# A two-layer graph transformer kernel: edge lags kept, one tile's output products moved, first loads re-ordered

## The chip, the core and the metric

The kernel runs on one core of a Trainium2 chip. The core has five engines that run side by side, each through its own list of instructions in order: TensorE (PE, matrix products into the accumulators in PSUM), VectorE (DVE), ScalarE (ACT), GpSimd (POOL) and SyncE (SP). SP, ACT and POOL also start DMA transfers between the chip's memory and the on-chip buffer SBUF. An engine waits for another through semaphores.

The metric is the device time of one execution in microseconds (us). Three executions of the kernel before took 2208.89, 2213.21 and 2214.76 us; the median is 2213.21.

## The reference, cut to what matters

There are 625 nodes of 1024 features and 10000 edges. Each of two layers normalises the nodes, adds a graph part and a linear attention to them, and then adds a feed-forward part. All that the change touches lies in layer 0:

```python
edge_index = jnp.stack([src, dst])
xn = _layernorm(x, axis=-1)
x = x + _L0_gnn_ref(xn, edge_index, L0_gnn_rms_w, ...) + _L0_mix_ref(xn[None], L0_mix_W_q, ...)[0]
x = x + _L0_ffn_ref(_layernorm(x, axis=-1)[None], L0_ffn_w_gate, ...)[0]
xn = _layernorm(x, axis=-1)
...
# _L0_gnn_ref: attention along the edges, 4 heads of 64
xl = (x @ Wl).reshape(n, H, D)
xr = (x @ Wr).reshape(n, H, D)
msg = xl[src] + xr[dst]
act = jnp.where(msg > 0, msg, NEG_SLOPE * msg)
e = jnp.einsum('ehd,hd->eh', act, att)
m = jax.ops.segment_max(e, dst, num_segments=n)
p = jnp.exp(e - m[dst])
denom = jax.ops.segment_sum(p, dst, num_segments=n)
alpha = p / (denom[dst] + 1e-16)
out = jax.ops.segment_sum(alpha[..., None] * xl[src], dst, num_segments=n)
return out.reshape(n, HID) @ W_up
# _L0_mix_ref: linear attention, 16 heads of 64
kv = jnp.einsum('bhnd,bhne->bhde', kf, v)
denom = jnp.einsum('bhnd,bhd->bhn', qf, ksum) + EPS
out = jnp.einsum('bhnd,bhde->bhne', qf, kv) / denom[..., None]
return out.transpose(0, 2, 1, 3).reshape(B, N, D_MODEL) @ W_o + b_o
```

## The kernel before

**Tiles.** The 625 nodes are five tiles of 125 rows. Nodes transposed (`xnT`, `oT`) have features on the partitions in eight chunks of 128. Weights of 1024 x 1024 come in halves of 512 columns, and a `Half` (L113) loads one half as two transfers of 1 MB on SP's queue. The pool `wpool` has six such 1 MB buffers. The engines' order is the order in which the program calls them: nothing is scheduled afterwards. `Stream` (`do`, L174) only delays: what follows a product on DVE or ACT (`after`) is recorded when the next product is asked for.

**Opening.** The rows of x are loaded by SP, and W_down, then the left and right weights of the edge attention. ACT starts the loads of src, dst, rms_w and att at once. For each tile DVE normalises (`norm`, L485), PE transposes and makes the down product, and ACT writes the left and right rows (`xlr`) to the memory buffers `xl_d` (started by ACT) and `xr_d` (started by POOL). `root` (L496) makes a scale with a square root on ACT between two small DVE steps. A buffer `table` in memory takes one value per head for every pair of nodes, and SP fills it with zeros from a constant (6160 KB). The key and value weights of layer 0 come after these zeros in SP's order. A transfer that SP or ACT starts takes one of eight completion counters, in turn, and before it starts waits until the last transfer on that counter has landed. So a transfer on one queue can wait for one on another.

**Edges.** The 10000 edges stand 128 at a time in 79 columns, in 40 groups of two columns (the last has one of 16). For a column, POOL gathers the left rows (`ga`, by src) and the right rows (`gb`, by dst), DVE adds and scores them (`score_group`, L596), ACT raises them to exponentials, and POOL scatters the column to `table` (`scatter`, L605). Every scatter waits for the one before it to land, as both write `table`. The rows wait in five buffers on each side.

**Beats.** These steps are laid among the attention's products by a clock of estimated PE time: every product calls `work(us)`, and once enough has passed a beat is recorded (`one_beat`, L663). In beat g POOL gathers group g, DVE scores group g − 4, ACT raises g − 5 and POOL scatters g − 6 and g − 7's rest; these are the `lags` 4, 5, 6 (L650). The first six beats are 5.2 us apart, the others 8.5. Beats 5 to 9 also make the self loops of a tile and store them in the table's diagonal. Between two scatters of a beat stand gathers.

**Attention, layer 0.** First keys and values (L0_Wk, L0_Wv), with a product that counts edges into a matrix `CT` between them; then per 128 columns m a query product and, one step later, `answer` (L327): two products `pd`, `po`, and on DVE a sum, a reciprocal and a multiplication into `oT`. In the last two steps of that loop all lags are lowered by one each time. `mixed(t)` (L718) makes tile t's products with W_o, two halves of eight chunks, into a two-bank accumulator `px1` of the tag `ps2`, which has three buffers. Tile 0's first six chunks are made before the last answer. Then tiles 3 and 4 are finished and kept in SBUF (`kept`, with the bias), and 0, 1 and 2 stay in their accumulators. On the way DVE sums and rounds the feed-forward weights to three values (`weight_sums`, `ternary`).

**Tile periods.** When all edges are scattered, `load_table` (L807) reads the table's columns of a tile back (started by POOL, 1.25 MB), `weigh` multiplies them with `CT` on DVE, `sums` makes the weighted sums on PE, `up_again` multiplies with W_up into the tile's accumulator (for tiles 3 and 4 into a fresh one) and DVE adds that to x. The loop over p (L1025) overlaps this for tile p with the feed-forward of tile p − 1 (`ffn`) and, from p = 2 on, with layer 1's key and value products as spacers. Before it POOL starts the load of table tile 0, of all five row tiles of x, and of table tile 1. SP's loads of layer 1's key and value weights stand at p = 1.

Of the kernel before, what the change touches and what calls it, by code (L numbers as in the profile page):

```python
# [21 lines left out]
P = 125  # L22
NP = 626
HN = 313
E = 10000
# [28 lines left out]
def attempt(ctx: ExitStack, tc: tile.TileContext, w: dict, out: bass.AP, shifted: bool):  # L54
# [161 lines left out]
    class LinearAttention:  # L216
# [17 lines left out]
        def half(self, c, loaded=False):  # L234
            Wk, bk, Wv, bv = (w[n] for n in self.names[1:])
            self.bk, self.bv = self.bias(bk, c, "bk_t"), self.bias(bv, c, "bv_t")
# [107 lines left out]
    with ExitStack() as st0:  # L344
# [8 lines left out]
        with ExitStack() as edges:  # L353
# [10 lines left out]
            for dst, name in ((si, "src"), (di, "dst")):  # L364
                flat = w[name].rearrange("a b -> (a b)")
                nc.scalar.dma_start(out=dst[:, 0:EF], in_=flat[0:128 * EF].rearrange("(p t) -> p t", t=EF))
                nc.scalar.dma_start(out=dst[0:ER, EF:EN], in_=flat[128 * EF:E].rearrange("(p t) -> p t", t=1))
# [5 lines left out]
            for t in range(2, NT):  # L373
# [5 lines left out]
            nc.scalar.dma_start(out=att, in_=w["att"].to_broadcast([128, 256]))  # L379
# [5 lines left out]
            nc.gpsimd.memset(none, FAR if shifted else 0.0)  # L385
            nc.sync.dma_start(out=table.rearrange("(p a b) h -> p a (b h)", p=128, a=28),
                              in_=none.unsqueeze(1).to_broadcast([128, 28, 440]))
            sf = pool.tile([128, EN], FP, name="sf")
# [5 lines left out]
            def edge_numbers():  # L394
                for dst, src in ((sf, si), (df, di)):
                    nc.vector.memset(dst[:, EF:EN], -1.0)
                    nc.vector.tensor_copy(dst[:, 0:EF], src[:, 0:EF])
                    nc.vector.tensor_copy(dst[0:ER, EF:EN], src[0:ER, EF:EN])
# [11 lines left out]
            if not shifted:  # L410
                nc.vector.tensor_scalar(att, att, 0.8, None, op0=ALU.mult)
# [128 lines left out]
            turn_x(1)  # L540
            root(0)
            for t in range(NT):
# [9 lines left out]
                if t == NT - 2:  # L552
# [4 lines left out]
            lin = LinearAttention(xnT, ("L0_Wq", "L0_Wk", "L0_bk", "L0_Wv", "L0_bv"), w["L0_bq"],  # L557
                                  lambda us: work(us), nc.sync)
            lin.half(0)
# [121 lines left out]
            def work(us):  # L681
                beat["us"] += us

                while beat["us"] >= 2.0 + 5.2 * min(beat["g"], 6) + 8.5 * max(beat["g"] - 6, 0) and chunks:
# [33 lines left out]
            def mixed(t, ks=range(KC), keep=None, then=None):  # L718
                for c in range(2):
# [15 lines left out]
                    work(0.87 * len(ks))  # L735
# [29 lines left out]
            for m in range(KC):  # L765
                if m >= KC - 2:
# [1168 lines left out]
```

## Time and profile before

| | |
|---|---|
| three executions, median | 2213.21 us (2208.89 to 2214.76) |
| the profiled execution, whole | 2212.67 us |
| its span, first to last instruction | 2210.6 us |
| PE busy | 2119.9 us (96%) |
| DVE, ACT, POOL busy | 714.3, 194.3, 342.3 us |
| mean granted clock of PE | 0.978 |
| first gather on POOL | 53.47 us |
| last scatter on POOL | 409.18 us |
| load of the first table tile issued | 414.73 us |
| first table product on DVE | 424.29 us |

Times in the views are us from the span's start. A row of the order of time gives start, duration, engine, line, operation, output and input with their shapes; in brackets stand the engine's idle time before it and what ended that. A row of the waits gives the engine and what it was about to do, then who released it, then total, number and longest. The granted clock is the share of full speed that PE was given. A busy PE is not a PE at its peak, since matrix products are pipelined. An f32 product of one chunk is two records.

### The profile page before, as it was taken

What the parts mean: (1) busy time and instruction counts of PE and PEld (TensorE: products, weight loads), DVE (VectorE), ACT (ScalarE), POOL (GpSimd) and SP (SyncE); (2) the same over time, 40 slices, a digit from 0 to 9 for tenths busy, and PEclk for the clock granted to TensorE, in tenths of its full rate; (3) what the DMA queues carried; (4) which work ended last, traced back from release to release, by engine and by line L of the source; (5) the groups of instructions that cost most, each with busy time, mean ns of one, the idle gap of its engine ahead of it and who ended that gap; (6) DMA issues with size and microseconds to landing.
All of it is one profiled execution on the core that took longest, in us unless ns stands there. A gap on an engine that the chain in (4) does not pass through costs nothing. (4 is left out here: it accounts for less than half of the span.)

```text
span 2210.6 us, 17366 instructions
## 1 busy us (share of the span) xinstructions
PE 2119.9 (96%) x6934; PEld 1215.4 (55%) x6934; DVE 714.3 (32%) x1216; ACT 194.3 (9%) x354; POOL 342.3 (15%) x351
## 2 busy tenths in 40 slices
PE   7999997869899989999999999999999999999998
PEld 5665573445455667754446767457744444444443
DVE  4786486467421760000122133322011111111012
ACT  2010110002211200000000111100000000000000
POOL 1666776400000120010000000110000000000011
PEclk9999999869999999999999999999999999999999
DMA  9335432620122110240213111122099988997742
GB/s 293 92 98 180 146 113 79 161 66 22 44 80 76 48 48 1 76 161 20 76 38 105 38 39 38 29 95 94 8 361 345 331 306 295 330 330 285 275 143 92
DMA packets 145849, 301.62 MB, mean 136 GB/s; under 512 B 12371, under 2 KB 22437, under 8 KB 145755
## 3 DMA queue, kind: packets, MB, share of 16 engines
q1 hardware_dynamic: 123412, 243.18, 31.0%
q0 software_dynamic: 17664, 47.47, 7.1%
q10 hardware_dynamic: 4678, 9.72, 1.4%
q8 instruction: 58, 0.95, 0.2%
q14 instruction: 37, 0.30, 0.0%
HBM read 277.49 MB, written 22.84 MB: 136 GB/s over the span
## 5 line engine op out<-in xcount | busy, mean ns | idle before, releaser
L130 PE MATMUL pu<-w,xgT 128*128 128x512 f32 x768 | 333.9, 593 | 1.9 <-DVE xgT L1229 1.9
L130 PEld LDWEIGHTS pu<-w,xgT 128*128 128x128 f32 x768 | 144.0, 190 | 174.8 <-issue 171.9
L130 PE MATMUL pyb<-w,hb 128*128 128x512 f32 x384 | 174.3, 598 | 2.5 <-ACT yb L105 2.1
L130 PE MATMUL pk<-w,xnT 128*125 128x512 f32 x320 | 143.9, 603 | 3.8 <-DMA w<-in_L_Wk_dram 3.2
L130 PE MATMUL pv<-w,xnT 128*125 128x512 f32 x320 | 141.2, 594 | 0.0
L130 PE MATMUL pq<-xnT,w 128*128 128x313 f32 x512 | 138.1, 428 | 2.0 <-ACT qf L320 1.2
L130 PE MATMUL p<-tT,w 128*128 128x313 f32 x512 | 136.3, 428 | 0.4 <-DVE tT L1229 0.4
L130 PEld LDWEIGHTS pyb<-w,hb 128*128 128x128 f32 x384 | 69.8, 189 | 90.9 <-issue 74.8
L130 PEld LDWEIGHTS pq<-xnT,w 128*128 128x128 f32 x512 | 96.5, 190 | 42.1 <-ACT qf L320 3.7
L1769 DVE TENSOR_TENSOR su<-pu,su 128x512 f32<-128x512 f32 x24 | 16.6, 692 | 314.6 <-ACT su L1768 314.6
L130 PEld LDWEIGHTS p<-tT,w 128*128 128x128 f32 x512 | 96.8, 190 | 37.9 <-issue 1.2
L130 PEld LDWEIGHTS pk<-w,xnT 128*125 128x125 f32 x320 | 60.3, 191 | 77.8 <-issue 76.0
L130 PEld LDWEIGHTS pv<-w,xnT 128*125 128x125 f32 x320 | 60.0, 189 | 72.4 <-issue 71.8
L610 POOL DMA_INDIRECT table<-es,at x79 | 83.9, 1062 | 63.2 <-issue 33.7
L1752 POOL DMA_INDIRECT xg<-rows_d,slots x12 | 11.4, 947 | 524.7 <-PE pxg L1759 449.0
L592 POOL DMA_INDIRECT ga<-xl_d,si x79 | 82.3, 1041 | 29.6 <-issue 19.8
L592 POOL DMA_INDIRECT gb<-xr_d,di x79 | 78.9, 998 | 24.1 <-issue 23.5
L724 PE MATMUL px<-w,oT 128*125 128x512 f32 x160 | 71.1, 605 | 11.3 <-DVE z L337 11.3
L1119 DVE TENSOR_TENSOR z<-pz,z 125x512 fp32r<-125x512 f32 x10 | 6.9, 692 | 196.8 <-ACT z L1117 196.8
L130 PE MATMUL px<-w,hT 128*125 128x512 f32 x160 | 70.3, 592 | 0.0
L130 PE MATMUL px<-w,oT 128*125 128x512 f32 x160 | 70.3, 592 | 0.0
L130 PE MATMUL ph<-meanT,w 128*128 128x313 f32 x256 | 70.0, 426 | 0.0
(368 smaller groups left out, 2538.9 us busy)
## 6 DMA issues: line engine op xcount, KB each, us to landing
w<-in_eW_dram SPq DMA_DIRECT2D x144, 1024.0 KB
w<-in_L_Wk_dram SPq DMA_DIRECT2D x8, 1024.0 KB
w<-in_L_Wv_dram SPq DMA_DIRECT2D x8, 1024.0 KB
w<-in_L_Wq_dram SPq DMA_DIRECT2D x8, 1024.0 KB
w<-in_L_Wo_dram SPq DMA_DIRECT2D x8, 1024.0 KB
w<-in_W_self_dram SPq DMA_DIRECT2D x8, 1024.0 KB
w<-in_W_neigh_dram SPq DMA_DIRECT2D x8, 1024.0 KB
w<-in_sW_dram SPq DMA_DIRECT2D x8, 1024.0 KB
```

The source lines that it names most:

```text
L130: nc.tensor.matmul(dst, lhsT=lhsT, rhs=rhs, start=(i == 0), stop=(i == len(pairs) - 1))
L592: nc.gpsimd.indirect_dma_start(out=ab[g][side][0:p, j, :], out_offset=None, in_=src[:, :], in_offset=bass.IndirectOffsetOnAxis(ap=ix[0:p, ...
L610: nc.gpsimd.indirect_dma_start(out=table[:, :], out_offset=bass.IndirectOffsetOnAxis(ap=at[0:p, lo + j:lo + j + 1], axis=0), in_=es[0:p, l ...
L724: nc.tensor.matmul(hold["px", t][:P, c, :], lhsT=oT[:, k, nodes(t)], rhs=wo[c](k), start=(k == 0), stop=(k == KC - 1 and keep is not None))
L1119: nc.vector.tensor_tensor(low, src, high.bitcast(FP), op=ALU.subtract)
L1752: nc.gpsimd.indirect_dma_start(out=xg, out_offset=None, in_=rows_d[:, :], in_offset=bass.IndirectOffsetOnAxis(ap=slots[:, b:b + 1], axis=0))
L1769: nc.vector.tensor_tensor(su, pu[:, 0, :], su, op=ALU.mult)
```

## The change

- `LinearAttention` for layer 0 is made earlier, and its biases and key weights are loaded ahead of the table's zeros, the value weights behind them (`biases`, and `half` with `biased`).
- The loads of src, dst and att (ACT's queue) move from the start behind the second tile's transpose (`load_edges`), and DVE's scaling of att into `edge_numbers`.
- A beat after the sixth is 8.1 us of estimated time instead of 8.5.
- The lags stay at 4, 5, 6 to the end of the loop over m, and are then set to 1, 1, 2 as before. Tile 0's six chunks before the last answer call no `work`.
- `kept` holds tile 3 only. Tile 0's last two chunks come right behind tile 3, and tile 4's products move to p = 1, one half before the sums of tile 1 and one after the table product of tile 2. They stay in an accumulator until p = 4, and tile 4's bias is added to x.
- Layer 1's first key and value weights are asked for behind the second half of these products.
- The second table tile is loaded behind the first row tile instead of the fifth.

```diff
+        def biases(self, c):
+            self.bk, self.bv = (self.bias(w[self.names[i]], c, tag) for i, tag in ((2, "bk_t"), (4, "bv_t")))
+
+        def half(self, c, loaded=False, biased=False):
+            if not biased:
+                self.biases(c)
...
-            for dst, name in ((si, "src"), (di, "dst")):
-                flat = w[name].rearrange("a b -> (a b)")
-                nc.scalar.dma_start(out=dst[:, 0:EF], in_=flat[0:128 * EF].rearrange("(p t) -> p t", t=EF))
-                nc.scalar.dma_start(out=dst[0:ER, EF:EN], in_=flat[128 * EF:E].rearrange("(p t) -> p t", t=1))
...
-            nc.scalar.dma_start(out=att, in_=w["att"].to_broadcast([128, 256]))
+
+            def load_edges():
+                for dst, name in ((si, "src"), (di, "dst")):
+                    flat = w[name].rearrange("a b -> (a b)")
+                    nc.scalar.dma_start(out=dst[:, 0:EF], in_=flat[0:128 * EF].rearrange("(p t) -> p t", t=EF))
+                    nc.scalar.dma_start(out=dst[0:ER, EF:EN], in_=flat[128 * EF:E].rearrange("(p t) -> p t", t=1))
+                nc.scalar.dma_start(out=att, in_=w["att"].to_broadcast([128, 256]))
...
+            lin = LinearAttention(xnT, ("L0_Wq", "L0_Wk", "L0_bk", "L0_Wv", "L0_bv"), w["L0_bq"],
+                                  lambda us: work(us), nc.sync)
+            lin.biases(0)
+            lin.wk = Half(wpool, w["L0_Wk"], 0)
             nc.sync.dma_start(out=table.rearrange("(p a b) h -> p a (b h)", p=128, a=28),
                               in_=none.unsqueeze(1).to_broadcast([128, 28, 440]))
+            lin.wv = Half(wpool, w["L0_Wv"], 0)
...
             turn_x(1)
+            load_edges()
             root(0)
...
-            lin = LinearAttention(xnT, ("L0_Wq", "L0_Wk", "L0_bk", "L0_Wv", "L0_bv"), w["L0_bq"],
-                                  lambda us: work(us), nc.sync)
-            lin.half(0)
+            lin.half(0, loaded=True, biased=True)
...
-                while beat["us"] >= 2.0 + 5.2 * min(beat["g"], 6) + 8.5 * max(beat["g"] - 6, 0) and chunks:
+                while beat["us"] >= 2.0 + 5.2 * min(beat["g"], 6) + 8.1 * max(beat["g"] - 6, 0) and chunks:
...
-            def mixed(t, ks=range(KC), keep=None, then=None):
-                for c in range(2):
+            def mixed(t, ks=range(KC), keep=None, then=None, paced=True, cs=(0, 1)):
+                for c in cs:
...
-                    work(0.87 * len(ks))
+                    if paced:
+                        work(0.87 * len(ks))
...
             for m in range(KC):
-                if m >= KC - 2:
-                    lags[:] = [n - 1 for n in lags]
                 if m + 1 < KC:
                     lin.query(m + 1)
                 else:
-                    mixed(0, range(6))
+                    mixed(0, range(6), paced=False)
...
-            kept = mid([P, 2, 2, 512], "kept")
-            mixed(3, keep=kept[:, 0], then=weight_sums)
-            mixed(4, keep=kept[:, 1])
+            kept = mid([P, 2, 512], "kept")
+            mixed(3, keep=kept, then=weight_sums)
+            mixed(0, range(6, KC))
             weight_means()
-            mixed(0, range(6, KC))
...
-            kept_apart = t >= 3
+            kept_apart = t == 3
...
             rows_dma(nc.gpsimd, x[:, t, :], xrows[t])
-        load_table(1)
+            if t == 0:
+                load_table(1)
...
             if p == 1:
-                lin1.weights(0)
+                mixed(4, cs=(0,))
...
-                    nc.vector.tensor_tensor(xc, xc, bo[c][:P] if t < 3 else kept[:, t - 3, c, :], op=ALU.add)
+                    nc.vector.tensor_tensor(xc, xc, kept[:, c, :] if t == 3 else bo[c][:P], op=ALU.add)
             if p == 1:
+                mixed(4, cs=(1,))
+                lin1.weights(0)
                 lin1.half(0, loaded=True)
```

More of the change, by code (lines that the diff above doesn't have):

```diff
@@ L232, in weights @@
             self.wk, self.wv = (Half(wpool, w[self.names[i]], c) for i in (1, 3))
-        def half(self, c, loaded=False):
-            Wk, bk, Wv, bv = (w[n] for n in self.names[1:])
-            self.bk, self.bv = self.bias(bk, c, "bk_t"), self.bias(bv, c, "bv_t")
+        def biases(self, c):
[3 more added lines that the diff above has]
+                self.biases(c)
             if not loaded:
@@ L394, in edge_numbers @@
             def edge_numbers():
+                if not shifted:
+                    nc.vector.tensor_scalar(att, att, 0.8, None, op0=ALU.mult)
                 for dst, src in ((sf, si), (df, di)):
@@ L409, in attempt @@
             nc.vector.memset(xl1[:, :, :, 64:65], 1.0)
-            if not shifted:
-                nc.vector.tensor_scalar(att, att, 0.8, None, op0=ALU.mult)
             counting = [(lo, hi, t) for lo, hi in (((0, 27), (27, 53), (53, EN)) if shifted else ((0, EN),))
```

## The prediction

> **What bounds the kernel now.** I read the time slices of the page first. TensorE (PE) is near nine tenths or more from about 600 us to the end, so anything won must come from the first 600 us.
>
> ```profile
> PE   7999997869899989999999999999999999999998
> PEclk9999999869999999999999999999999999999999
> ```
>
> The seventh to ninth slices (332 to 497 us) are the bad place: PE has gaps, and its granted clock drops. The view of busy time by stage gives sizes (columns: length, then PE, weight load, DVE, ACT and POOL busy with counts, granted clock, DMA share, GB/s).
>
> ```profile
> 340.00:360.00 20.00, 8.71 (x22) 4.23 (x21) 10.92 (x16) 0.63 (x3) 14.06 (x14) 0.79 0.20 52
> 400.00:420.00 20.00, 19.02 (x45) 8.06 (x43) 7.88 (x10) 0.00 (x0) 9.75 (x11) 1.00 0.50 156
> 420.00:440.00 20.00, 12.10 (x44) 9.89 (x45) 5.59 (x8) 1.66 (x2) 5.70 (x10) 0.59 1.05 253
> 460.00:480.00 20.00, 11.93 (x32) 6.13 (x32) 15.44 (x31) 3.31 (x4) 2.33 (x5) 0.72 0.33 89
> ```
>
> The waits of PE over the first 800 us name what ended its gaps.
>
> ```profile
> PE pg L130 <- DVE pT L821: 12.0, 10, 6.4
> PE px L724 <- DVE z L337: 11.3, 1, 11.3
> PE pk L130 <- DMA w<-in_L_Wk_dram: 3.2, 1, 3.2
> ```
>
> So three gaps: the first key product waits 3.2 us for its weights, the output products wait 11.3 us for the last head's answer, and the graph sums wait for the table of edge scores. The last is the one that counts, and what feeds it is POOL. The order of time on POOL at its tail, then DVE's two table products:
>
> ```profile
> 391.17 0.86 POOL L592 DMA_INDIRECT gb<-xr_d,di  x1 [0.30 <-issue]
> 392.33 1.00 POOL L610 DMA_INDIRECT table<-es,at  x1 [0.30 <-DMA table<-es,at]
> 395.25 0.96 POOL L610 DMA_INDIRECT table<-es,at  x1 [1.91 <-ACT es L579]
> 397.62 1.38 POOL L610 DMA_INDIRECT table<-es,at  x1 [1.41 <-DMA table<-es,at]
> 400.87 1.85 POOL L610 DMA_INDIRECT table<-es,at  x1 [1.87 <-issue]
> 404.11 2.32 POOL L610 DMA_INDIRECT table<-es,at  x1 [1.40 <-DMA table<-es,at]
> 409.18 0.85 POOL L610 DMA_INDIRECT table<-es,at  x1 [2.75 <-issue]
> 414.73 0.89 POOL L164 DMA_DIRECT2D tb<-table  x1 [4.70 <-DMA table<-es,at]
> ```
>
> ```profile
> 424.29 4.83 DVE L821 TENSOR_TENSOR pT<-tb,CT 125x500 f32<-125x500 f32 x5 [16.21 <-DMA tb<-table]
> 447.16 4.83 DVE L821 TENSOR_TENSOR pT<-tb,CT 125x500 f32<-125x500 f32 x5 [10.14 <-DMA tb<-table]
> ```
>
> POOL issues 237 gathers and scatters from 53.5 us on. It is busy 15.4 of 20 us with 16 of them wherever nothing holds it, so one takes 1.27 us and POOL is full. DVE waits for no gather before 345 us. PE ends its work at 419.0 and then stands until the table lands: **the end of POOL's stream sets the time, PE's own gaps before it don't**.
>
> **What the Trainium skill says.** "DMA: Bandwidth & Descriptors", Issuing engines are not separate DMA queues: transfers of all issuing engines share the same 16 DMA engines. The trace agrees: the table load (1.25 MB) took 9.56 us to reach DVE while 4 MB of weights from SP's queue ran, DMA share 1.0. "SBUF — State Buffer", SBUF: two separate sides, says that GpSimd can't write descriptors while a DVE operation holds the shared ports. The trace fits: scatters took 1.38 to 2.32 us during the ternary rounding on DVE (396.3 to 407.5 us), against 0.95 to 1.0 before. "TensorE: Matmul & The Clock Gate", Part 1: half clock after an idle window of some 3.4 us, full again after a busy one. The first key group took 10.12 us after its gap, later ones 7.03.
>
> **The change, part by part.**
>
> *Opening.* Key weights go ahead of the table's zeros (6.16 MB). Removed: the 3.17 us wait and 10.12 − 7.03 = 3.1 us of half clock, 6.3 us together. Five loads (src, dst, att) move on ACT's queue from the start to behind tile 1's copy: 0.41+0.44+0.45+0.45+0.57 = 2.3 us, now ahead of the square root of `root(0)`, for which DVE waits before `norm(2)`. SP, whose second row load waited 3.3 us for src, no longer does, so W_down lands some 3 us sooner; the two cancel, and tile 2's transpose stays at 19 us. SP's Wk now waits for att's completion (its counter is re-used), about 18 us; 2.5 MB at 370 GB/s (25 to 31 us) lands by 27, long before 45. The zeros then land at 44 to 46 instead of 40.3, and tile 4's last left-row write waits for that counter. Before, DMA ran at 160 GB/s for 6 us after the zeros (37 to 44 us) because SP waited; that hole closes, so the first gather (53.47) comes 2 to 5 us sooner. The first scatters wait for the self-loop stores (91.9 to 121.5 us, 9.4 us of waits), which follow PE and DVE, so POOL's stream ends up about 6 us earlier. Bounds: 2, as the gather's start alone, and 8, with the pace's 1.2 to 1.6 us.
>
> *Pace 8.5 to 8.1.* A beat g comes 0.4(g − 6) us earlier in DVE's order. POOL is full, so it can't follow; DVE then waits at a score for its gather. The margins between landing and score are 2 to 10 us from group 15 on, so I expect waits of up to 6 us. They delay PE a few us, which the stall before the table hides; without that cover they'd cost some 5 us.
>
> *Lags kept.* The built order has no score group left between the last head's product and its answer (before: two), so the 11.3 us gap and about 3.5 us of half clock go. PE is 15 us earlier, for nothing while POOL sets the end. But POOL's order changes too. Before, from 341.56 (second gather of group 34) to the last gather at 391.17: 34 transfers in 49.6 us, 1.46 each, since a scatter waits for the one before it to land and only one gather lay between. Now 30 transfers with two gathers between, 1.28 each: 38.4 us, 11.2 less. In return ten scatters, not six, follow the last gather back to back. Free spacing is 2.4 us (395.25 to 397.62), under the rounding 3.25, 3.25, 5.07. The six took 16.9 us; the ten take 3 spacings under the rounding (11.6) and 6 × 2.4, 26.0 us: 9.1 more. Net −2 us; bounds −6.5 (all at 2.4) and +1.2 (all at 3.25).
>
> *L1 weights after the moved products.* Before, key weights were issued at 408.75, beside the last scatter, whose successor came 5.6 us later instead of about 3: −2.5. The load then takes 1.25 MB at 250 GB/s plus 2.2 us landing, 7.2 instead of 9.56: −2.4; bounds −1 and −4.
>
> Sum so far, first table product: −6 −2 −2.5 −2.4 = **−12.9 us**.
>
> *Second table load behind the first row tile.* It waited behind five row loads and landed for 447.16. Now 1.75 MB later than the first, 7 us; DVE is free for it 12.7 us after the first product begins, before 22.9: DVE gains 10 us.
>
> *Tile 4's output products in the second period.* 32 records × 0.43 = 13.8 us of PE, 27.5 at half clock, leave a place where they hid behind POOL and fill one where PE idles: 18.3 us of its waits from 444.8 to 495. The first half starts when DVE has read tile 0's accumulator (21.7 us after the first table product begins). Part cold, it takes 7 to 10 us, and the graph sums of tile 1 end at 33 to 38 us instead of 34.7. So the 10 us are spent here. The second half lies under the rounding and gate chain of DVE (4.1 us idle) and `weigh(2)`. In return PE is warm: the sums of tile 2 took 8.66 us against 4.58 warm. Tile 4 now holds one of three two-bank accumulators: 1 us for the first down product, which waits for tile 1's addition, 0.7 later. Net **−3 us**; bounds −8 and +6. The two additions to `kept` that go (1.4 us of DVE) and the bias added later lie off the path.
>
> Sum: −16. The profiled execution took 2212.67 us (span 2210.6), 0.5 below the median 2213.21: 2212.7 − 16 = 2196.7, so **2197**. After 500 us nothing changes in kind, and PE is bound, so the gain stays.
>
> **Rivals.**
> (a) *The scatter tail eats the opening*: ten scatters, each held by the one before and by DVE, 3.25 us or more apart, and the gathers start only 2 us sooner. The table is asked for at −2 +1.2 −2.5 = −3, lands −5.5 and with −2 in the second period: 2205. For it: 400.87 to 409.18. Against: spacing was 2.4 without the rounding.
> (b) *More than forecast*: POOL follows the opening fully (−8), tail −6.5, load −6, and PE stays warm from the first period on (−7): 2185. Against it: half clock held from 425 to 445 though PE was nearly continuous.
> (c) *The moved products land on the path* (slower): at half clock they need 27.5 us against 18.3 us of gaps: +9. With a table only 3 us sooner, 2219. It decides when PE time added in period two beyond its gaps exceeds what the table gained. Against: a long product stream is what warms the clock.
> (d) *The kept lags don't help*: certain for PE's gap, as said; it is in my sum.
>
> **How the numbers follow.** Main case 0.56 (own range 2190 to 2203), (a) 0.19, (b) 0.17, (c) 0.08. The range 2185 to 2208 reaches to (a) and (b) and leaves (c). No-change is within 0.3% (6.6 us), about what measurement can tell. Faster: main, (b) and over half of (a), 0.84; same 0.09; slower 0.07.
>
> **What would show it.** Right: no wait of `pk` for Wk; z's gap below 2 us; PE standing 15 to 30 us for the first table product, so a longer gap there than the 6.4 us now; that product at 409 to 414; ten scatters after the last gather; the second table product right after tile 0's sums; moved products at 0.43 us a record at least in their second half. Wrong: a first gather later than 53 us, scatters 3 us apart throughout, or a second period longer than 50 us.

## The result, and the profile after

The changed kernel takes 2209.02 us (median; 2205.55 to 2216.21), the kernel before 2214.63 us beside it. The ratio is 0.9980, with a 95% interval of 0.9972 to 0.9988: 4.4 us faster by the ratio and 5.6 by the medians, where 16 were forecast. The profiled span went from 2210.6 to 2205.7 us.

The time slices of the page after, as they were shown of before:

```profile
PE   7999999489899989999999999999999999999998
PEclk9999999689999999999999999999999999999999
```

The slices from the second to the seventh are full now; the eighth (386 to 441 us) fell to four tenths. The view of busy time by stage (length, then PE, weight load, DVE, ACT, POOL, granted clock, DMA share, GB/s) shows the same: PE is full at 340 us, and idle from 400 to 420.

```profile
340.00:360.00 20.00, 20.00 (x50) 9.07 (x49) 19.42 (x13) 0.21 (x1) 15.12 (x17) 1.00 0.23 67
400.00:420.00 20.00, 0.00 (x0) 0.00 (x0) 0.49 (x1) 0.00 (x0) 9.67 (x14) 0.54 0.37 93
420.00:440.00 20.00, 16.79 (x50) 11.51 (x50) 12.34 (x18) 1.66 (x2) 4.58 (x9) 0.53 0.90 223
```

The waits of PE over the first 800 us: the gap of 11.3 us for `z` is gone, and so is the wait of 3.2 us for Wk at the first key product (the 0.8 us below stand at a later one, at 163.86 us). What PE won, and the 14 us of tile 4's products that left this place, stand now as a wait in front of the table's first product.

```profile
PE pg L130 <- DVE pT L828: 24.9, 5, 23.8
...
PE pk L130 <- DMA w<-in_L_Wk_dram: 0.8, 1, 0.8
```

POOL's order of time at its tail, and then DVE's products with the first and the second table:

```profile
380.33 0.86 POOL L601 DMA_INDIRECT gb<-xr_d,di  x1 [0.30 <-issue]
381.50 1.00 POOL L619 DMA_INDIRECT table<-es,at  x1 [0.30 <-DMA table<-es,at]
384.40 2.26 POOL L619 DMA_INDIRECT table<-es,at  x1 [1.90 <-ACT es L588]
388.05 2.33 POOL L619 DMA_INDIRECT table<-es,at  x1 [1.39 <-DMA table<-es,at]
392.30 1.81 POOL L619 DMA_INDIRECT table<-es,at  x1 [1.91 <-DMA table<-es,at]
395.51 0.96 POOL L619 DMA_INDIRECT table<-es,at  x1 [1.40 <-DMA table<-es,at]
398.36 0.96 POOL L619 DMA_INDIRECT table<-es,at  x1 [1.90 <-issue]
...
408.79 0.85 POOL L619 DMA_INDIRECT table<-es,at  x1 [1.91 <-DMA table<-es,at]
411.40 0.89 POOL L164 DMA_DIRECT2D tb<-table  x1 [1.76 <-DMA table<-es,at]
```

```profile
419.51 4.83 DVE L828 TENSOR_TENSOR pT<-tb,CT 125x500 f32<-125x500 f32 x5 [23.75 <-DMA tb<-table]
432.16 4.85 DVE L828 TENSOR_TENSOR pT<-tb,CT 125x500 f32<-125x500 f32 x5
```

The last gather is 10.8 us sooner (391.17 to 380.33). The forecast had 11.2 for the order at the tail and 6 more for the opening; these 6 are missing. The 138th of the 158 gathers goes out at the same time in both kernels, so all of the 10.8 us comes from the last twenty, which have 13 scatters among them in place of 17 (first row before, second row after):

```profile
336.35 0.95 POOL L592 DMA_INDIRECT gb<-xr_d,di  x1 [0.30 <-issue]
336.40 0.95 POOL L601 DMA_INDIRECT gb<-xr_d,di  x1 [0.30 <-issue]
```

Ten scatters follow the last gather in place of six, as forecast, and they use all of it: the last scatter moved from 409.18 to 408.79. The first table product moved from 424.29 to 419.51, and the three parts of these 4.8 us can be read off: 0.4 us from the last scatter's start, 2.9 from there to the table's load (5.55 to 2.61), and 1.45 from the load (9.56 to 8.11).

So the new opening gave POOL's stream nothing. ACT's order of time around the last left-row write, then POOL's first gather:

```profile
46.59 0.31 ACTq L164 DMA_DIRECT2D xl_d<-xlr  x1
51.04 0.31 ACTq L165 DMA_DIRECT2D xl_d<-xlr  x1
51.38 1.28 ACT L258 ACT_TABLE_LOAD   x1 [4.82 <-DMA table<-none]
```

```profile
56.32 1.18 POOL L601 DMA_INDIRECT ga<-xl_d,si  x1 [8.18 <-issue]
```

The second part of tile 4's write stood 4.4 us behind the first, because its completion counter was last taken by the table's zeros, and these landed at 51 us. The first gather came 2.85 us later than in the profile before, but two single profiles mislead here: in the three other profiles with the old opening (opening_undone, before_weights_late and before_lags_kept, below) it stands at 56.1 to 57.3 us, and in the eight with the new one at 54.9 to 57.7. What all eight show is that second part, 2.8 to 6.6 us behind the first, where 0.35 us is usual. At the 61st of the 79 scatters the four profiles with the old opening stand at 352.9 to 354.4 us, the eight with the new one at 350.8 to 359.7: no gain.

From the first table product to the quantised transposes of the third period (p = 2) it is 67.9 us, before 70.7: another 2.8 us. So the third period starts at 487.39 instead of 495.01. From there to the end it is 1718.3 us here and 1715.6 before. That is no property of the change: over the eighteen profiles of this study it lies anywhere from 1715.4 to 1722.7, with the same work in it. One place where such time goes is eight feed-forward products at 572 us, which took 3.57 us here and 1.94 before: the granted clock was 0.57 here and 1.00 there, behind the same wait of 2.7 us. So the part behind the third period's start is left out where profiles are compared below, and whole kernels are compared by the timed ratio.

### The profile page after: what moved, and what is told of

It reads as the page before. It is cut to its first block, busy times and chain, and to the rows that moved or that the text cites. A ratio compares the mean times of both kernels' runs of the same rounds, so it can differ in the third digit from the quotient of the medians.

```text
span 2205.7 us, 17365 instructions
## 1 busy us (share of the span) xinstructions
PE 2112.0 (96%) x6934; PEld 1209.6 (55%) x6934; DVE 714.3 (32%) x1214; ACT 194.2 (9%) x354; POOL 342.3 (16%) x351
## 5 line engine op out<-in xcount | busy, mean ns | idle before, releaser
L130 PEld LDWEIGHTS pk<-w,xnT 128*125 128x125 f32 x320 | 59.4, 188 | 72.8 <-issue 70.7
L733 PE MATMUL px<-w,oT 128*125 128x512 f32 x160 | 71.4, 604 | 5.3 <-DVE kept L739 4.0
```

The costliest lines, as they stand in the source:

```text
L130: nc.tensor.matmul(dst, lhsT=lhsT, rhs=rhs, start=(i == 0), stop=(i == len(pairs) - 1))
L733: nc.tensor.matmul(hold["px", t][:P, c, :], lhsT=oT[:, k, nodes(t)], rhs=wo[c](k), start=(k == 0), stop=(k == KC - 1 and keep is not None))
```

## The experiments

All kernels in one table, us from the span's start. "Second" and "third" are counted from the first table product: to the second tile's table product, and to the third period's transposes.

| kernel | last gather | last scatter | first product | second | third | third starts at | ratio to before (95%) |
|---|---|---|---|---|---|---|---|
| before | 391.2 | 409.2 | 424.3 | 22.9 | 70.7 | 495.0 | |
| after | 380.3 | 408.8 | 419.5 | 12.7 | 67.9 | 487.4 | 0.9980 (0.9972 to 0.9988) |
| opening_undone | 381.6 | 410.0 | 420.9 | 12.7 | 67.3 | 488.2 | 0.9983 (0.9976 to 0.9990) |
| lags_undone | 386.2 | 412.3 | 422.8 | 12.7 | 66.6 | 489.4 | 1.0004 (0.9995 to 1.0013) |
| pace_undone | 392.1 | 410.6 | 421.5 | 12.7 | 67.4 | 488.9 | 0.9962 (0.9947 to 0.9977) |
| second_table_late | 381.0 | 409.4 | 420.2 | 15.3 | 71.4 | 491.6 | 1.0002 (0.9992 to 1.0013) |
| values_ahead_of_zeros | 378.8 | 407.3 | 418.1 | 12.7 | 68.1 | 486.3 | 0.9973 (0.9963 to 0.9983) |
| rounding_other_form | 381.3 | 411.5 | 422.7 | 12.7 | 66.4 | 489.2 | 0.9988 (0.9979 to 0.9997) |
| tile4_before_table | 378.1 | 410.9 | 422.7 | 12.7 | 61.3 | 484.0 | 0.9966 (0.9952 to 0.9981) |
| tile4_and_weights_early | 386.7 | 419.7 | 431.5 | 12.7 | 61.8 | 493.3 | 0.9978 (0.9966 to 0.9990) |
| weights_behind_table | 381.1 | 409.1 | 419.8 | 12.7 | 62.6 | 482.4 | 0.9963 (0.9950 to 0.9976) |
| before_weights_late | 390.3 | 408.4 | 419.6 | 16.2 | 65.1 | 484.8 | 0.9950 (0.9935 to 0.9965) |
| before_lags_kept | 391.6 | 415.0 | 426.1 | 16.1 | 65.1 | 491.2 | 0.9982 (0.9967 to 0.9996) |
| combined | 383.3 | 409.4 | 420.4 | 12.7 | 60.5 | 480.8 | 0.9949 (0.9935 to 0.9962) |

Each ratio is to executions of the kernel before in the same session; before_weights_late has only four of its own, the others five to twenty.

Single profiles spread. Five of these kernels (after, second_table_late, weights_behind_table and the two with tile 4's products early) are the same program up to the 61st scatter, and yet have it at 353.1, 353.9, 354.1, 350.8 and 359.7 us. So a few us in the first three columns are not read by themselves. What is read is the order of POOL's transfers, steps inside one profile, and times from the first product: the six kernels that leave the second period as it is in the changed kernel have the third at 66.4 to 68.1.

### The opening

opening_undone puts the first loads back:

```diff
+                nc.scalar.dma_start(... src, dst, att ...)    # at the start, load_edges() gone
-            lin.biases(0); lin.wk = Half(...)                 # ahead of the zeros
+            lin.half(0)                                       # biases, key and value weights behind
```

> The changed kernel with its opening alone put back: src, dst and att loaded first, zeros ahead of the key weights. Theory S (the stores of the self-loops re-time GpSimd, so what happens ahead of about 92 us is forgotten): first gather back at 53.5 us instead of 56.3, but the first scatter still at 91 to 92.5, the last scatter within 1.5 us of the changed kernel's 408.8, first table product within 1.5 us of 419.5, time within 0.1% of the changed kernel. Rival F (the first gather's start carries through): last scatter and time 2.5 to 3 us sooner than changed. Rival P (PE's 6.3 us at the opening reach the scatters, as the forecast had it): last scatter 4 to 6 us later.

Measured: the ratio stays (0.9983 against 0.9980). PE's key products begin at 49.33 us, 3.7 later than in the changed kernel, and yet the last scatter came only 1.2 us later, which is within the spread. Rival P, which asked for 4 to 6, is out. Theory S and rival F both start from a first gather back at 53.5 us; it came at 57.34, so neither is tested.

The three further profiles with the old opening also show that the loss which the forecast wanted to remove was not always there. In the profile before, PE waited 3.17 us for the first key weights, and the group behind that wait took 10.12 us, at a granted clock of 0.50 from 49 to 52 us. Here it did not wait, and the group took 7.03 us; in before_weights_late and before_lags_kept it was:

```profile
48.35 7.10 PE L130 MATMUL pk<-w,xnT 128*125 128x512 f32 x16 [0.79 <-DMA w<-in_L_Wk_dram]
48.84 7.10 PE L130 MATMUL pk<-w,xnT 128*125 128x512 f32 x16
```

values_ahead_of_zeros takes the last left-row write off the zeros' counter:

```diff
-            nc.sync.dma_start(out=table..., in_=none...)
             lin.wv = Half(wpool, w["L0_Wv"], 0)
+            nc.sync.dma_start(out=table..., in_=none...)
```

> The changed kernel with the value weights moved ahead of the table's zeros too; by this the last left-row write of ScalarE no longer shares its completion counter with the zeros. Theory C (that shared counter is what holds the first gather): the write is issued at 46 to 47 us instead of 51.0, first gather 49 to 52, first scatter 35 us behind it or, if the self-loops bind first, at 86 to 89; last scatter 3 to 5 us sooner than 408.8, time 3 to 5 us below the changed kernel's. Rival C2 (the zeros' traffic itself slows the landing of the rows): first gather at 54 or later. Rival S (the self-loops re-time GpSimd at 91 to 92 us whatever came first): gather early, but first and last scatter within 1.5 us of the changed kernel's.

Its ACT, first gather and first scatter:

```profile
45.95 0.31 ACTq L164 DMA_DIRECT2D xl_d<-xlr  x1
46.30 0.43 ACTq L165 DMA_DIRECT2D xl_d<-xlr  x1
```

```profile
53.37 1.03 POOL L601 DMA_INDIRECT ga<-xl_d,si  x1 [5.85 <-issue]
...
88.77 1.19 POOL L619 DMA_INDIRECT table<-es,at  x1 [0.31 <-issue]
```

Theory C holds for the start: the write does not wait, and the first gather is 2.95 us sooner than in the changed kernel and sooner than in all eight profiles with the wait. It is not at the 49 to 52 us hoped for, as 7 us still pass between the last write and the gather. combined, with the same order of loads, has no wait either, and its first gather at 54.80 us. The first scatter follows the first gather by 35.4 us, as in the changed kernel (35.6). How much of this reaches the table stays open: the last scatter is 1.5 us sooner than in the changed kernel, which is within the spread, and the time is 0.9973 against 0.9980, where 3 to 5 us less were expected; the intervals overlap.

### Lags and pace

lags_undone puts the lowering back (and the pacing of tile 0's first products), pace_undone the 8.5 us, both in the changed kernel. before_lags_kept keeps the lags in the kernel before:

```diff
+                if m >= KC - 2:                               # lags_undone
+                    lags[:] = [n - 1 for n in lags]
...
-   ... + 8.1 * max(beat["g"] - 6, 0) and chunks:              # pace_undone
+   ... + 8.5 * max(beat["g"] - 6, 0) and chunks:
```

> The changed kernel with the lowered lags of the last two heads put back (and the paced first products with them). Theory T (a scatter in the tail costs what two gathers in between would have saved): last gather back near 390, some 10 us later than the changed kernel's 380.3, last scatter at 408 to 410, first table product within 1.5 us of 419.5; the gap of PE ahead of the output products is back at 9 to 12 us and costs nothing; time within 0.1% of the changed kernel. Rival (the kept lags are worth 2 us and more, as forecast): last scatter at 411 or later. Rival (the kept lags hurt): last scatter before 407.

> The changed kernel with the pace of its beats alone put back (8.5 us of PE's work to a beat behind the sixth, instead of 8.1). Theory (GpSimd is full, so it can't follow a faster pace): last gather and last scatter within 1.5 us of 380.3 and 408.8, time within 0.1% of the changed kernel's. Rival (the faster pace feeds the stream): last scatter 2 us and more later, time 2 to 4 us above. Rival (the faster pace makes DVE wait for gathers, PE and the scores with it): last scatter 2 us and more sooner.

> The kernel before with its lags kept until the last head's answer and the first products unpaced, and nothing else; tile 4's products stay ahead of the table. Theory L (the kept lags bring the last gather sooner and end PE's work 10 to 14 us sooner, so layer 1's weights now leave in the middle of the scatters): last gather 379 to 383 instead of 391.2, ten scatters behind it, key weights leave at 396 to 402 instead of 408.75, the scatter behind them takes 5 to 6 us, last scatter 410 to 413 instead of 409.2; table load no longer slowed; first table product 422 to 425, time within 0.15% of before. Rival (kept lags alone are worth 3 us and more): last scatter before 407, time 3 us and more below before.

With the changes crossed, the pace makes most of the tail, and the kept lags add to it only with the fast pace. With 8.5 us six scatters follow the last gather whether the lags are lowered (before) or kept (pace_undone, before_lags_kept), and it comes at 391 to 392 us; the expectations of both had it some 10 us sooner and failed. With 8.1 us it comes sooner, at 386.2 with nine scatters behind it (lowered) or 380.3 with ten (kept). A faster beat leaves fewer groups for the catching-up, in which a scatter stands behind every gather: seven such groups at 8.5, three in the changed kernel. The end of POOL's stream is about the same either way, 408.8 us in the changed kernel and 410.6 in pace_undone.

With the fast pace the kept lags (and the unpaced first products) are worth something: undoing them costs 0.0024 of the time, some 5 us and clear of the intervals, where no more than 0.1% was expected. Undoing the pace is faster by the times (0.9962), which its one profile does not show (third period at 488.9, not 487.4). The intervals overlap, so whether 8.1 was a gain or a loss stays open.

before_lags_kept shows what kept lags alone would do. SP's weights for layer 1 and POOL's tail:

```profile
396.29 3.81 SPq L121 DMA_DIRECT2D w<-in_L_Wk_dram  x2
```

```profile
402.23 1.72 POOL L610 DMA_INDIRECT table<-es,at  x1 [3.20 <-DMA table<-es,at]
409.73 0.96 POOL L610 DMA_INDIRECT table<-es,at  x1 [5.79 <-issue]
412.09 0.96 POOL L610 DMA_INDIRECT table<-es,at  x1 [1.40 <-DMA table<-es,at]
```

PE ended its output products sooner, so the buffers came free at 396 us, the weights left among the scatters, and one scatter came 7.5 us behind the last, where 2.4 is usual. The rounding on DVE ran beside it until 406.3 us and has a part in this: in before_weights_late, where no weights are near, one step under the rounding takes 4.98 us. The last scatter was 5.8 us later than before.

### Where tile 4's products and the weights go

```diff
+            mixed(3, keep=kept[:, 0], then=weight_sums)       # tile4_before_table
+            mixed(4, keep=kept[:, 1])
...
             if p == 1:
-                mixed(4, cs=(0,))
+                lin1.weights(0)                               # ..._and_weights_early
+                lin1.weights(0, nc.gpsimd)                    # weights_behind_table
```

> The changed kernel with tile 4's output products back ahead of the graph sums and kept in SBUF; layer 1's weights stay late. Theory M (the moved products spend what the earlier second table gives): first table product within 1.5 us of 419.5, second 12.7 us after it, and the quantised transposes of the third period 4 to 8 us sooner than the changed kernel's 487.4, so a time 4 to 8 us below the changed kernel's. Rival (they lie in gaps of PE): the third period's start within 1.5 us of 487.4 and the time within 0.1%.

> As the kernel with tile 4's output products ahead of the table, and layer 1's key and value weights asked for at their old place as well, when the last output products end (about 409 us). Theory W (these weights are what held the last scatter's landing and the table load): table asked for 2.5 to 4 us later than there, load 9 to 10 us instead of 8.1, first table product 4 to 5 us later, time 4 to 5 us above that of the kernel with late weights. Rival (the table came sooner for the stream's sake): first table product within 1.5 us of the other kernel's.

> As the kernel with tile 4's output products ahead of the table, but layer 1's key and value weights asked for from GpSimd's queue, in program order behind the loads of the first tables, so that they can't run beside the last scatters. (In the kernel with SP's queue they had left at 398.0 us, when the last output products end, and the scatter after them came 6.1 us later, where its neighbours have 2.4 to 2.9.) Theory W (these 4 MB hold the landing of the scatters and of the table): from the last gather to the last scatter 26 to 28 us instead of 32.8, table load 7 to 8 us, time 5 to 6 us below the kernel with SP's queue, that is 0.9935 to 0.9945 of before. Rival (the scatters were slow for another reason): tail still above 31 us and the time within 0.1% of that kernel's.

Theory M holds: without the moved products the third period starts 61.3 us behind the first product, not 67.9, so they cost 6.6 us there. The time is lower by some 3 us (0.9966 against 0.9980; the intervals overlap), not by 4 to 8. The edit also did more than it says. SP has nothing else to do, so its place in the program doesn't hold the weights; the buffers do (its wait ends with PE's output products `px`), and with tile 4's products done early these came free at 398 us. POOL and SP of tile4_before_table:

```profile
398.02 3.81 SPq L121 DMA_DIRECT2D w<-in_L_Wk_dram  x2
```

```profile
398.00 0.96 POOL L619 DMA_INDIRECT table<-es,at  x1 [1.63 <-DMA table<-es,at]
404.10 0.96 POOL L619 DMA_INDIRECT table<-es,at  x1 [5.14 <-issue]
407.17 0.96 POOL L619 DMA_INDIRECT table<-es,at  x1 [2.11 <-DMA table<-es,at]
410.93 0.85 POOL L619 DMA_INDIRECT table<-es,at  x1 [2.80 <-DMA table<-es,at]
```

These three steps took 12.9 us; in the changed kernel the last three take 8.1. So tile4_and_weights_early does not differ from it in kind (its weights left at 406.8), and its late table has another source too: its 61st scatter, up to which the programs are the same, was already 6.6 us late. Its ratio is 0.0012 above, with intervals that overlap: nothing is read from it. weights_behind_table is the clean test: its tail is 28.0 us, not 32.8 (expected 26 to 28). Its time did not follow (0.9963 against 0.9966, expected 0.9935 to 0.9945): a miss in size; the intervals still leave room for half of the expected gain.

before_weights_late is the same single edit in the kernel before.

```diff
             if p == 1:
-                lin1.weights(0)
+                lin1.weights(0, nc.gpsimd)
```

> The kernel before, with one edit: layer 1's key and value weights are asked for from GpSimd's queue behind the first table loads instead of from SP's. Theory W (the weights beside the last scatter and the table load cost 5 us): last scatter at 408 to 410.5, table asked for 2.5 to 3.5 us behind it instead of 5.55, first table product some 8 us behind that instead of 9.56; together the product comes 4 to 5.5 us sooner after the last scatter than before (15.1 us there), time 4 to 5 us below before (0.9977 to 0.9982). Rival (the landing is slow for the scatters' own sake): product 14 us and more behind the last scatter, time within 0.1% of before.

Its last scatters, the table's load and DVE's table products:

```profile
408.36 0.85 POOL L610 DMA_INDIRECT table<-es,at  x1 [2.66 <-issue]
410.96 0.90 POOL L164 DMA_DIRECT2D tb<-table  x1 [1.75 <-DMA table<-es,at]
```

```profile
419.62 4.83 DVE L821 TENSOR_TENSOR pT<-tb,CT 125x500 f32<-125x500 f32 x5 [12.28 <-DMA tb<-table]
435.85 4.91 DVE L821 TENSOR_TENSOR pT<-tb,CT 125x500 f32<-125x500 f32 x5 [3.48 <-DMA tb<-table]
```

The load is asked for 2.6 us behind the last scatter (5.55 before) and the product follows 8.7 us later (9.56): 3.8 us by these, and 4.7 with the last scatter. That much was expected. The time fell by twice that, 0.9950. The rest is in the second period: the second table arrives 16.2 us behind the first product, not 22.9, with its load still behind all five row tiles, and the third period starts 65.1 behind it, not 70.7. So the 4 MB of weights had held back the second table as well. before_lags_kept, whose weights went out at 396 us, shows the same: 16.1 and 65.1.

### The second table, and the rounding

```diff
-            if t == 0:                                        # second_table_late
-                load_table(1)
+        load_table(1)                                         # behind the loop
...
-   nc.vector.tensor_scalar(v, v, wscale, 1.0, ...)            # rounding_other_form, all three passes
+   nc.vector.scalar_tensor_tensor(v, v, wscale, one, ...)
```

> The changed kernel with the second table load back behind all five row tiles. Theory: first table product within 1.5 us of 419.5, the second 20 to 23 us after it instead of 12.65, the third period's quantised transposes 3 to 6 us later than 487.4, time 3 to 6 us above the changed kernel's. Rival (tile 4's products fill PE in that time, so DVE's earlier start is worth nothing): third period within 1.5 us, time within 0.1%.

The third period starts 71.4 us behind the first product, 3.5 more, and the time is 0.0022 higher, some 5 us: the theory holds. The second product comes 15.3 us behind the first, however, not 20 to 23, as the weights are out of the way.

> The changed kernel with the nine passes of the ternary rounding written as scalar_tensor_tensor against a broadcast column instead of tensor_scalar: the same values, but a form that runs at half the rate (about 2.1 us a pass instead of 1.23). Theory D (it is the fast form of DVE that keeps GpSimd from issuing): scatters in the tail at 2.4 to 2.9 us throughout, none above 3, GpSimd's issues at 0.96 us; last scatter 3 to 4 us sooner, time 3 to 4 us below the changed kernel's. Rival (any DVE work slows it): spacings above 3 us over 19 us instead of 11, last scatter 2 to 4 us later.

Theory D falls: three of the nine steps are above 3 us (4.0 to 4.2), as with the fast form (3.2 to 4.3). POOL and DVE:

```profile
385.38 2.83 POOL L619 DMA_INDIRECT table<-es,at  x1 [1.89 <-ACT es L588]
```

```profile
385.03 2.33 DVE L774 SCALAR_TENSOR_TENSOR raw<-raw,wscale,row 128x2048 f32<-128x2048 f32 x1
387.40 2.29 DVE L775 SCALAR_TENSOR_TENSOR raw<-raw,row 128x2048 f32<-128x2048 f32 x1
```

The slow form (2.3 us a pass instead of 1.23 to 1.28) holds POOL as the fast one does: the scatter that began at 385.38 ended only in the second pass. The tail took 30.2 us instead of 28.5, as the rival had it in kind, though its steps above 3 us come to 12 us and not 19; the times do not tell them apart (0.9988 against 0.9980, the intervals overlap). The Trainium skill's page "SBUF — State Buffer", SBUF: two separate sides, fits this: it names, beside the fast forms, operations with two SBUF inputs, against a GpSimd operation that reads SBUF. Whether a scatter's issue is such an operation, no run here shows.

### Put together

combined is weights_behind_table with the values ahead of the zeros, and with two of three rounding passes on ScalarE behind the last scores:

```diff
+                nc.scalar.activation(v, v, AF.Identity, bias=far[:, 0:1], scale=wscale[:, i:i + 1])
+                nc.scalar.activation(v, v, AF.Identity, bias=far[:, 1:2], scale=1.0)
+                nc.vector.tensor_scalar(m, v..., 1.0, -1.0, op0=ALU.min, op1=ALU.max)
```

> The changed kernel with tile 4's output products back ahead of the table, layer 1's weights on GpSimd's queue behind the first table loads, value weights ahead of the zeros, and the ternary rounding behind the last scores: two of its three passes (the scaling and rounding, and the subtraction) on ScalarE, the clip on DVE. Each theory as measured so far: first gather 53 us, ten scatters in 24 to 25.5 us instead of 27.3 to 28.5 as only three DVE passes are left to stretch them, last scatter 404 to 406.5, first table product 415 to 417.5, third period 61 to 63 us behind it, time 0.9935 to 0.9950 of before. Rival (ScalarE's 14 us of passes end too late for the first table's buffer): table asked for more than 4 us behind the last scatter, time no better than 0.9963.

Its tail is 26.0 us (expected 24 to 25.5), its last scatter later than expected (409.35, as the last gather came 3 us late), its third period the soonest of all, at 480.8. Only two of its scatters are stretched (1.57 and 1.43 us, beside DVE's passes); beside ScalarE's they take 0.96. It takes 0.9949 of before: it beats both kernels, but so does before_weights_late, with one edit and 0.9950.

Two further kernels, each measured twice, asked what late weights give with the early second table alone, and whether the combined kernel gains from the pace of 8.5:

> The kernel before with two edits: layer 1's weights on GpSimd's queue behind the first tables, and the second table load behind the first row tile. Theory (late weights give the table 4.7 us and, as they leave the second table load alone too, 5.6 us in the second period; an earlier second table then adds what is left of DVE's wait): last scatter 408 to 410, first table product 419 to 421, second 12.7 us behind it instead of 16.2, third period 61 to 63 us behind the first product instead of 65.1, time 2 to 4 us below the kernel with late weights alone (0.9930 to 0.9945). Rival (the second period is then bound by PE's cold clock and DVE's chain): third period 64 to 66 us behind the first product, time as with late weights alone (0.9945 to 0.9955).

> The kernel with late weights and the early second table (nothing else of the change) once more, since the chip of the first try stopped all engines for 10 to 25 us at several places of the stage that is to be measured. Theory as before: last scatter 408 to 410, first table product 419 to 421, second 12.7 us behind it, third period 61 to 63 us behind the first product, time 0.9930 to 0.9945 of before. Rival: third period 64 to 66 us behind the first product, time 0.9945 to 0.9955.

> The combined kernel with the pace of 8.5 us instead of 8.1. The order that the pace leaves on GpSimd has seven groups of edges in which each gather has a scatter behind it, and six scatters behind the last gather (three and ten with 8.1). Theory (a scatter behind a gather costs 1.27 us, one behind a scatter 2.4 to 2.9, but the earlier scatters wait for scores; the two cancel): last gather 390 to 393, last scatter within 1.5 us of the combined kernel's 409.35, time within 0.15% of its 0.9949. Rival (fewer scatters in a row save 1 us each): last scatter 404 to 407, time 0.993 or less.

> The combined kernel with the pace of 8.5 us once more, for the same reason. Theory as before (the two orders cancel): last gather 390 to 393, last scatter within 1.5 us of the combined kernel's 409.35, time 0.9935 to 0.9965 of before. Rival (fewer scatters in a row save 1 us each): last scatter 404 to 407, time 0.993 or less.

Both times the kernel before itself took 2.5% more than otherwise (2270.7 and 2267.7 us), and PE stood between single products for nothing that the profile shows, 29 to 42 us in all ahead of the first table product (0 in before, 1.3 us in the changed kernel). The last scatter came at 460 us and later. In combined_old_pace_again at 88 us:

```profile
87.99 1.01 PE L130 MATMUL pv<-w,xnT 128*125 128x512 f32 x1 [1.58 <-issue]
89.39 1.01 PE L130 MATMUL pv<-w,xnT 128*125 128x512 f32 x1 [0.39 <-issue]
```

Late weights with the early table took 0.9967 (0.9949 to 0.9985) and 0.9956 (0.9939 to 0.9973). Combined with the old pace took 1.0013 (1.0001 to 1.0025) and 1.0018 (0.9995 to 1.0040). That all engines stopped for 10 to 25 us in the first try, as the expectation of two_edits_again says, its trace does not show: no stretch without work on any engine is longer than 4.4 us. As the delays fall on the very stage under study, these ratios are not set against the others, and the pace stays open. From the first table product on PE has no such stand. The third period starts 59.6 us behind it in before_weights_late_table_early and 62.8 in two_edits_again, where 61 to 63 was expected and 65.1 is what late weights give alone.

## Why the prediction was wrong in size

It said 2197 (2185 to 2208); 2209 came. The first table product came 4.8 us sooner instead of 12.9, the third period 7.6 instead of 16. Most of the mechanisms came as described; one term of the sum, the opening, gave nothing.

- **Opening (−6 us on POOL's stream): failed.** This is the largest part of the miss. "The zeros then land at 44 to 46" and the first gather "comes 2 to 5 us sooner": they landed at 51, the last left-row write waited for their counter in all eight profiles, and the first gather stands where it stands with the old opening (54.9 to 57.7 us, and 53.5 to 57.3). The shared counter was in the forecast; the landing was sized without the value weights and the row writes that run beside 6 MB of zeros, though no run shows which of them made it late. The size also rested on one execution. The wait of 3.17 us and the group of 10.12 us stand in the profile before alone; in the three other profiles with the old opening PE waited 0.8 us or less, the group took 7.03 to 7.10 us, and POOL's waits up to its eighth scatter, beyond the usual 0.3 us a transfer, were 4.0 to 4.3 us in place of 8.1. PE starts its keys at 44.7 to 45.7 us with the new opening and at 48.4 to 49.3 with the old one, but POOL did not follow: giving that back (opening_undone) leaves the time as it is.
- **Its sign of being wrong,** a first gather later than 53 us, came. By itself it says little, as all four profiles with the old opening have it too.
- **Pace (nothing): half right.** What it does to the time stays open, but the early last gather and the ten scatters, which the forecast put down to the kept lags, need it.
- **Lags and tail (−11.2 + 9.1 = −2 us).** The two sizes were near: −10.8, and the ten scatters took 10.4 us longer than the six (27.3 against 16.9 us to the last issue). Net −0.4. That the two sizes came so near is in part luck, as they come from the lags and the pace together: with the slow pace kept lags leave the last gather at 391.6 us (391.2 before). With the fast one they are worth some 5 us of time.
- **Weights of layer 1 (−2.5 and −2.4): right, and the largest gain of the change.** Measured −2.9 and −1.45. What the forecast missed is that they held the second table too.
- **Second period (−3): right, by the runs as well.** By pairs of kernels, weights away −5.6 (70.7 to 65.1), second table sooner −3.5 (71.4 to 67.9), tile 4's products +6.6 (61.3 to 67.9); the sum is −2.5, and −2.8 was measured. The forecast gave the first two as one, 10 us from the order of the loads, and had the price of the products about right.
- **"After 500 us nothing changes" is true of the work,** but the span of that part varies by 7 us between profiles, about as much as the gain at the third period (7.6), so how much of it the time keeps (4.4 by the ratio) is not settled by profiles.

Of the rivals, (a) was nearest: its table asked for 3 us sooner (3.3 measured), though for other reasons than it gave. (c), tile 4's products on the path, holds for 6.6 us of cost, but with the table earlier it did not decide. (d), that the end of PE's gap is worth nothing by itself, was right: PE now stands 23.8 us for the table.

## What to carry to other kernels

When a transfer is given a later place in the program, ask what really holds it: here SP had nothing else queued, so free buffers set the time, and where PE ended sooner ahead of the table (before_lags_kept, tile4_before_table) 4 MB of weights went into the chain of scatters. Put such loads behind the transfers they must not meet, on the same queue; that one edit gave more (0.9950) than the whole change (0.9980). When a large transfer is moved, look up who takes its completion counter next, and when the transfer lands beside everything else that runs. And before a forecast rests on a wait, look whether a second execution of the same program has it: the 6 us of this one stood in one profile of four.

## What had not been expected of the hardware

- A scatter whose predecessor lands while 2 to 4 MB of weights are loaded comes up to 6.1 us behind it (tile4_before_table), and 7.5 with the rounding on DVE beside it (before_lags_kept), instead of 2.4 to 2.9.
- Executions of the same program differ by 9 us at the 61st scatter (350.8 to 359.7) and by 7 us behind the third period.
- A DVE pass of half the rate (2.3 us) stretches a scatter's issue on POOL to 2.6 to 2.8 us, as the faster pass (1.25 us) stretches it to 2.3; without either it is 0.96, also beside ScalarE's passes of 2.0 to 2.1 us (combined).
- PE's granted clock was 0.50 behind a wait of 3.17 us (49 to 52 us in before), and behind one of 2.70 us and 1.4 us of work (573 to 575 us in the changed kernel). Behind the same 2.70 us in before it stayed at 1.00. Both waits are shorter than the 3.4 us that the prediction quotes.
- Twice every kernel, the one before too, took 2.5% longer. The four profiles of these sessions have 29 to 42 us of stalls on PE that wait for nothing in the profile, all ahead of the first table product; from the third period to the end it was 1717.6 to 1722.6 us, inside the range of the others.
